# Gating of a mixture of experts on one core: fewer small instructions, one-hot sets ahead of turns, the last tile turned in pieces

## The chip, the cores and the metric

The kernel runs on one core of a Trainium2 chip. A core has a matrix engine, TensorE (PE, with its weight loads, PEld), a vector engine, VectorE (DVE), ScalarE (ACT), GpSimd (POOL), and SyncE (SP), which only issues DMA transfers here. Each engine works through its own queue in order. [...] The metric is the time of one execution on the device, in microseconds (us), lower is better.

## What is computed

Two layers on an input of 4 x 16 x 16 positions with 1024 channels, that is 1024 tokens, all in float32. Layer 0 is a lambda convolution (not touched here). Layer 1 is attention with 16 heads of 64 over each batch entry's 256 tokens, and behind it a mixture of 8 experts, to whose gating the change belongs:

```python
gate_logits = jax.nn.softmax(x @ gate_w + gate_b, axis=-1)
selected = (gate_logits >= THRESHOLD).astype(x.dtype)     # 0.1
weights = gate_logits * selected
wsum = jnp.sum(weights, axis=-1, keepdims=True)
weights = weights / jnp.where(wsum == 0, jnp.ones_like(wsum), wsum)
for e in range(E):                                        # 8 experts, 1024 x 1024 each
    out = out + weights[:, e:e + 1] * (x @ expert_w[e] + expert_b[e])
```

Here x is the layer norm of the attention's result, and the sum over the experts is added to that result.

## The kernel before

The 1024 tokens are eight row tiles of 128. The attention ends with an output projection, `project_out(t, j)`: for row tile t and column half j it runs eight matmul steps, one per 128 channels (each is two instructions on PE, since the data are float32), and then DVE adds the result to the tile `xs[t]` (L922). Between the steps the gating is woven in by hand. A counter, `chunks`, counts the steps: 9 to 16 belong to tile 3, 17 to 32 to tile 4, 33 to 48 to tile 5, 49 to 64 to tile 6, 65 to 80 to tile 7. The table `at_chunk` (L1357) says after which step which stages are emitted, as pairs (stage, tile). The order of each engine's queue is the order in which the program emits (`tc.manual_schedule()`).

The stages of a tile are:

- Stage 0, `normalise` (L1147): statistics on DVE, one square root on ACT; for tiles 0 to 5 ACT writes the normalised row, SP stores it to a scratch `rows` in DRAM and fetches it back as four quarters; for tiles 6 and 7 DVE writes it in two halves (L1166). SP also stores `xs[t]` to `out`.
- Stage 1, `turn_rows` (L1170): the row transposed. Tiles 0 to 5 by one DVE transpose of the quarters (L187), which waits for their DMA; tiles 6 and 7 by eight PE transposes into two PSUM banks and two ACT copies (L1179, L1180), and then an ACT copy and an SP store that put the row into `rows`.
- Stages 2 to 5 work on a batch of tiles at once: (0, 1, 2), (3, 4, 5), (6), (7). Stage 2, `gate_sums`: 16 PE instructions per tile and one DVE copy. Stage 3, `gate` (L1205): PE's `pg`, then on DVE the copy of the token numbers into `listed`, bias, maximum, and Exp on ACT. Stage 4, `thresholds` (L1228): ten small DVE instructions. Stage 5, `place` (L1243): on PE a prefix sum over tokens, `pp` (L1250, L1251), on DVE the place of each token in its expert's list.
- Stage 6, `entries_of` (L1264), for each tile: two sets of one-hot rows on DVE (`one0`, `one1`, L1268) and two products with token number and weight (`entry`, L1276), on POOL for tiles 0 to 5 and on DVE for 6 and 7. The buffers of each of these are two deep.
- Stage 7, `enter` (L1285): 16 PE instructions that add the tile's entries into the lists, which lie in two PSUM banks under the tag `sc`.

After step 80 the list of expert 0 alone is copied and spread over the partitions (`copy_lists`, `spread_lists`, `take_lists`), seven `warm` matmuls keep PE going (L1420), and stages 0 and 1 of tile 7 follow, with a load of the Exp table between them. Then tile 7 is put through expert 0 as a whole (`weighted`, the "dense" product, 16 steps), while stages 2 to 6 of tile 7 are emitted between its steps, and POOL gathers the rows of expert 0. During the first seven products of expert 0 (L1516) come stage 7 of tile 7, the copy of all lists, and after product 4 `last_lists` (L1429): the spreads `pc`, two counts `pn` and `pn0`, and DVE's copies into `gather`, `slot` and `add`. PSUM banks of the tags `mm` and `tr` are rings of three each; `pc`, `pn`, `pn0` and the odd products take theirs from `tr`. Then come the products of the other experts, and what is left over.

Of the kernel before, what the change touches and what calls it, by code (L numbers as in the profile page):

```python
# [32 lines left out]
F32 = mybir.dt.float32  # L33
# [6 lines left out]
P = 128  # L40
# [16 lines left out]
E = 8  # L57
# [12 lines left out]
def kernel(  # L70
# [1027 lines left out]
    with ExitStack() as gating:  # L1098
# [40 lines left out]
        nc.vector.memset(kept[:, 0, :], 0.0)  # L1139

# [6 lines left out]
        def normalise(t):  # L1147
# [10 lines left out]
            if t < NT - 2:  # L1158
                normalised(row, xs[t], mv[:, 0:1], rstd)
                nc.sync.dma_start(rows[ts(t, P), :], row)  # L1160
                row = l2w.tile([P, Q, C // Q], F32, tag="xg", name=f"quarters{t}")
                quarters_of(rows[ts(t, P), :].rearrange("n (f c) -> n f c", f=Q), row)
            else:
                for j in range(2):
                    half = slice(j * HALF, j * HALF + HALF)
                    nc.vector.tensor_scalar(row[:, half], xs[t][:, half], mv[:, 0:1], rstd, ALU.subtract, ALU.mult)  # L1166
# [3 lines left out]
        def turn_rows(t, row):  # L1170
# [5 lines left out]
            for j in range(2):  # L1176
                pt = tr(f"row{t}_pt{j}")
                for c in range(4):
                    nc.tensor.transpose(pt[:, ts(c, P)], row[:, (4 * j + c) * P : (4 * j + c + 1) * P], ident)  # L1179
                nc.scalar.copy(row_T[:, 4 * j : 4 * j + 4, :], pt.rearrange("p (c n) -> p c n", c=4))  # L1180
# [6 lines left out]
            return row_T  # L1187
# [17 lines left out]
        def gate(tiles, sums):  # L1205
# [3 lines left out]
            for i in range(n):  # L1209
                nc.tensor.matmul(pg[:, ts(i, E)], sums[:, ts(i, P)], quarters, start=True, stop=True)  # L1210
            listed = of_tiles("listed", n, E, 2)
            nc.vector.tensor_copy(
                listed[:, :, :, 0], token[:, tiles[0] : tiles[0] + n].unsqueeze(2).to_broadcast([P, n, E])
            )
            weight = listed[:, :, :, 1]
            top, fix, keep = of_tiles("g_top", n), of_tiles("g_fix", n), of_tiles("g_keep", n, E)
# [4 lines left out]
            if n == 1:  # L1221
                nc.scalar.activation(weight, weight, AF.Exp, bias=top)
            else:
                nc.vector.tensor_add(weight, weight, top.unsqueeze(2).to_broadcast([P, n, E]))
                nc.scalar.activation(weight, weight, AF.Exp)
            return listed, top, fix, keep

        def thresholds(listed, top, fix, keep):  # L1228
            weight = listed[:, :, :, 1]
            all_of = top.unsqueeze(2).to_broadcast([P, top.shape[1], E])  # L1230
            nc.vector.tensor_reduce(top, weight, AX.X, ALU.add)
            nc.vector.reciprocal(top, top)
            nc.vector.tensor_mul(weight, weight, all_of)
            nc.vector.tensor_scalar(keep, weight, THRESHOLD, None, ALU.is_ge)
            nc.vector.tensor_mul(weight, weight, keep)
            nc.vector.tensor_reduce(top, weight, AX.X, ALU.add)
            nc.vector.tensor_scalar(fix, top, 0.0, None, ALU.is_equal)
            nc.vector.tensor_add(top, top, fix)
            nc.vector.reciprocal(top, top)
            nc.vector.tensor_mul(weight, weight, all_of)  # L1240
            return listed, keep

        def place(tiles, listed, keep):  # L1243
# [11 lines left out]
            nc.vector.tensor_scalar(slot, keep, -1.0, 1.0, ALU.mult, ALU.add)  # L1255
            nc.vector.tensor_mul(slot, slot, from_end[:, t0 : t0 + n, :])
            nc.vector.tensor_add(slot, slot, pp.rearrange("p (n e) -> p n e", n=n))
            at = l2w.tile([P, 3, n, E], I32, tag="at", name=f"at{t0}", padded_shape=[P, 3, 3, E])
            nc.vector.tensor_copy(at[:, 0, :, :], slot)
            nc.vector.tensor_scalar(at[:, 1, :, :], at[:, 0, :, :], 31, None, ALU.bitwise_and)  # L1260
            nc.vector.tensor_scalar(at[:, 2, :, :], at[:, 0, :, :], 5, None, ALU.logical_shift_right)
            return at, listed

        def entries_of(t, i, at, listed):  # L1264
# [10 lines left out]
            for k in range(2):  # L1275
                (nc.vector if t >= NT - 2 else nc.gpsimd).tensor_mul(  # L1276
                    entry[:, :, k, :], column, listed[:, i, :, k].unsqueeze(2).to_broadcast([P, E, 32])
# [25 lines left out]
        def spread_lists(a, entries):  # L1303
            pc = tr(f"pc{a}").rearrange("p (e i s) -> p e i s", e=E, i=2)
# [32 lines left out]
        def stage(n, t):  # L1337
# [11 lines left out]
            elif n == 5:  # L1349
                placed[t] = place(tiles, *gated[t])  # L1350
            elif n == 6:
                entered[t] = entries_of(t, t - tiles[0], *placed[tiles[0]])
# [16 lines left out]
            46: ((6, 1),),  # L1369
            47: ((1, 4),),  # L1370
            48: ((7, 0), (6, 2)),
            50: ((7, 1), (0, 5)),
            53: ((7, 2),),
# [6 lines left out]
            74: ((3, 6), (6, 4)),  # L1380
            75: ((7, 3), (4, 6), (6, 5)),
            76: ((7, 4),),
            77: ((5, 6), (6, 6)),
            78: ((7, 5),),
# [24 lines left out]
        with tc.manual_schedule():  # L1409
# [6 lines left out]
            pc = spread_lists(0, entries)  # L1416
# [5 lines left out]
            load_table(AF.Exp)  # L1422
            take_lists(0, 1, pc)
            stage(1, NT - 1)

# [3 lines left out]
        def last_lists(entries):  # L1429
            take_lists(1, E, spread_lists(1, entries))  # L1430


            pn = tr("pn")
            nc.tensor.matmul(pn[:, :E], ones, kept[:, NT, :], start=True, stop=True)
            need = l2.tile([P, E], F32, tag="need", name="need")
            nc.vector.tensor_copy(need, pn[:, :E])
            pn0 = tr("pn0")
            nc.tensor.matmul(pn0[:, :2], ones, kept[:, NT - 1, :: E - 1], start=True, stop=True)
            nc.vector.tensor_scalar(need[:, :: E - 1], pn0[:, :2], float(LEFT), None, ALU.add)
# [150 lines left out]
        with tc.manual_schedule():  # L1590
            entries, last_rows = [], []
            last_row_T = two.tile([P, NC, P], F32, tag="last_row_T", name="last_row_T", bufs=1)
            nc.scalar.copy(last_row_T, turned_rows[NT - 1])
# [156 lines left out]
```

## Time and profile before

| | us |
|---|---|
| median of 3 runs | 1225.91 (1224.85 to 1229.62) |
| the profiled execution, its own time | 1227.45 |
| its span, first to last instruction | 1225.6 |
| busy, TensorE | 1208.7 |
| busy, VectorE | 721.4 |
| busy, GpSimd | 401.5 |
| busy, ScalarE | 203.8 |
| mean granted clock of TensorE | 0.997 of full |

The span has one profiled execution, with times from its start. Step 9 begins at about 657 us, step 65 ends at 714.6, step 80 at about 735.3; dense runs from 739.8 to 755.1, expert 0 from there. Busy time of an engine counts instructions at work; the idle time in front of an instruction is given with what released it. The end of a matmul is modelled, so a run of matmuls is drawn slightly longer than the next one's start would allow.

### The profile page before, as it was taken

To read this page: it belongs to the slowest core of one execution; us is meant where nothing else is said; L and a number is where in the kernel's file an instruction comes from. 1 tells how busy PE (TensorE), PEld (TensorE's weight loads), DVE (VectorE), ACT (ScalarE), POOL (GpSimd) and SP (SyncE) were. 2 spreads that over 40 slices of the span, in tenths; PEclk is the share of its full clock that TensorE was granted. 3 is DMA by queue.
4 is the path that set the end of the run, shared out by engine and by line. 5 is a ranking of instruction groups with operands and counts; after the bars stand their busy time and mean duration, and the time that the engine had idled before them with its cause. 6 is when DMAs were issued, how large, how long until landed. Compare 5 with 4: busy or idle time off the path is not lost.

```text
span 1225.6 us, 13283 instructions
## 1 busy us (share of the span) xinstructions
PE 1208.7 (99%) x4780; PEld 632.8 (52%) x4780; DVE 721.4 (59%) x1274; ACT 203.8 (17%) x502; POOL 401.5 (33%) x467
## 2 busy tenths in 40 slices
PE   9999999999999999999999999999999999999998
PEld 5444884778884444444444444444344334434443
DVE  5796636668332666565644567666566655565742
ACT  3310111111001222121311212101111111111110
POOL 1051351364000122222232116427443635363521
PEclk9999999999999999999999999999999999999999
DMA  9102014772201353525465646564855576556432
GB/s 349 27 1 69 18 44 123 248 251 94 69 9 60 104 172 104 170 95 181 147 213 192 206 172 238 143 185 95 246 158 141 109 230 182 144 138 180 98 82 55
DMA packets 94121, 169.77 MB, mean 139 GB/s; under 512 B 11968, under 2 KB 48848, under 8 KB 94048
## 3 DMA queue, kind: packets, MB, share of 16 engines
q1 hardware_dynamic: 73600, 108.49, 26.8%
q0 software_dynamic: 16144, 51.45, 17.3%
q10 hardware_dynamic: 4304, 8.91, 2.1%
q8 instruction: 40, 0.66, 0.2%
q14 instruction: 33, 0.27, 0.1%
HBM read 116.12 MB, written 48.50 MB: 134 GB/s over the span
## 4 chain that ended last, share of the span: by engine, by line
PE 87%; DMA 7%; DVE 3%; SPq 2%; issue 1%; ACT 1%; POOL 0%; DVEq 0%; POOLq 0%; ACTq 0%
PE p L1516 31%; PE pqk L665 15%; PE pv L665 7%; PE po L920 5%; PE pq_pair L400 4%; PE left L1558 3%; PE pq L319 3%; PE pT L510 3%; DMA ln_rows<-ln_rows 2%; PE pk L431 2%; PE sc L824 2%; PE pa L893 2%; PE rest L1572 2%; PE pv L538 2%; DMA quarters<-rows 1%; DMA s<-two_T 1%
## 5 line engine op out<-in xcount | busy, mean ns | idle before, releaser
L1041 POOL DMA_INDIRECT w_e_xg<-rows,gather x146 | 156.3, 1071 | 50.9 <-issue 41.4
L1516 PE MATMUL p<-w_e,A 128*128 128x512 f32 x368 | 163.2, 593 | 1.3 <-DVE slot L1328 1.3
L865 POOL TENSOR_TENSOR s_q<-s_q,total 128x128 f32<-128x128 f32 (+1 forms) x128 | 60.2, 506 | 276.5 <-DVE total L862 276.5
L920 PE MATMUL po<-w_p,y_T 128*128 128x512 f32 x256 | 116.8, 607 | 0.0
L1516 PEld LDWEIGHTS p<-w_e,A 128*128 128x128 f32 x368 | 69.6, 190 | 89.9 <-issue 89.0
L1064 POOL DMA_INDIRECT out_dram<-y,add x32 | 56.5, 1766 | 177.5 <-ACT y L1522 114.3
L1516 PE MATMUL p<-T,S 128*128 128x512 f32 x256 | 112.7, 593 | 0.0
L1522 ACT ACTIVATE y<-y,slot 128x512 f32<-128x512 f32 x64 | 46.2, 723 | 333.1 <-DVE y L1530 177.9
L665 PE MATMUL pqk<-ln,w_qk 128*128 128x512 f32 x192 | 85.7, 595 | 0.0
L1516 PEld LDWEIGHTS p<-T,S 128*128 128x128 f32 x256 | 48.6, 190 | 60.8 <-issue 60.5
L850 ACT ACTIVATE s_q<-sc,top 128x128 f32<-128x128 f32 (+1 forms) x128 | 52.1, 420 | 164.4 <-DVE top L846 140.6
L920 PEld LDWEIGHTS po<-w_p,y_T 128*128 128x128 f32 x256 | 47.6, 192 | 54.5 <-issue 53.5
L187 DVE STREAM_TRANSPOSE A<-w_e_xg 128x1024 f32<-128x1024 f32 x32 | 39.7, 1240 | 47.2 <-DMA w_e_xg<-rows,gather 47.2
L665 PEld LDWEIGHTS pqk<-ln,w_qk 128*128 128x128 f32 x192 | 36.1, 190 | 43.7 <-issue 41.9
L665 PE MATMUL pqk<-T,S_qk 128*128 128x512 f32 x128 | 57.8, 595 | 0.0
L1516 PE MATMUL p<-T,A 128*128 128x512 f32 x128 | 57.5, 592 | 0.0
L1516 PE MATMUL p<-w_e,S 128*128 128x512 f32 x128 | 57.5, 592 | 0.0
L665 PE MATMUL pv<-w_v,ln 128*128 128x256 f32 x192 | 43.7, 380 | 1.5 <-ACT ln L223 1.1
L319 PE MATMUL pq<-w_q,xn 128*128 128x512 f32 x96 | 44.5, 599 | 0.3 <-ACT xn L299 0.3
L1558 PE MATMUL left<-w_e,one 128*32 128x512 f32 x312 | 41.8, 593 | 0.0
L1516 PEld LDWEIGHTS p<-w_e,S 128*128 128x128 f32 x128 | 24.3, 190 | 30.6 <-issue 30.1
L1516 PEld LDWEIGHTS p<-T,A 128*128 128x128 f32 x128 | 24.3, 190 | 30.6 <-issue 30.1
(329 smaller groups left out, 1846.5 us busy)
## 6 DMA issues: line engine op xcount, KB each, us to landing
w_e<-in_expert_w_dram SPq DMA_DIRECT2D x12, 2048.0 KB, 15.2
s_rows<-s_q SPq DMA_DIRECT2D x32, 384.0 KB, 2.3
s_rows<-s_rows SPq DMA_DIRECT2D x128, 96.0 KB, 2.3
w_qk<-in_W_attnT_dram SPq DMA_DIRECT2D x8, 1024.0 KB, 5.4
w_e<-in_expert_w_dram ACTq DMA_DIRECT2D x4, 2048.0 KB, 9.5
xn<-in_xT_dram SPq DMA_DIRECT2D x8, 512.0 KB, 7.2
w_q<-in_Wq_dram SPq DMA_DIRECT2D x16, 256.0 KB, 7.3
x_at<-in_x_dram POOLq DMA_DIRECT2D x8, 512.0 KB
```

The lines of the kernel that those rows point to most:

```text
L187: nc.vector.transpose(row_T[:, :, :slots].rearrange("p c (g j) -> p g c j", j=32), row[:, : slots // 32, :].rearrange("p g (c i) -> p g c ...
L319: nc.tensor.matmul(pq, xn[:, c, ts(t, P)], w_q[kc][:, c, :], start=(c == 0), stop=(c == NC - 1))
L400: nc.tensor.matmul(bank, a[:, c, :], b[:, c, :], start=(c == 0), stop=(c == NC // 2 - 1))
L665: nc.tensor.matmul(bank, stationary(c), moving(c), start=(c == 0), stop=(c == NC // 2 - 1))
L850: nc.scalar.activation(blocks(h, qt), psc[:, h, cols].rearrange("p (b f i) -> p b f i", f=Q, i=32), AF.Exp, bias=top[:, qt, h : h + 1], sc ...
L865: nc.gpsimd.tensor_mul(blocks(h, qt), blocks(h, qt), total[:, qt, h : h + 1].unsqueeze(2).unsqueeze(3).to_broadcast([P, 1 + qt, Q, 32]),)
L920: nc.tensor.matmul(po, y_T[:, c, ts(t, P)], w_p[j][:, c, :], start=(c == 0), stop=(c == NC - 1))
L1041: nc.gpsimd.indirect_dma_start(out=row[:, g, :], out_offset=None, in_=table[: (TOK - P) * Q, :] if e in SHORT else table, in_offset=bass.I ...
L1064: nc.gpsimd.indirect_dma_start(out=out[: TOK - P, :] if e in SHORT else out, out_offset=bass.IndirectOffsetOnAxis(ap=add[:slots, e, k : k ...
L1516: nc.tensor.matmul(bank, a[:, c, :], b[:, c, :], start=(c == 0), stop=(c == NC // 2 - 1))
L1522: nc.scalar.mul(y[i][:, ts(j, HALF)], y[i][:, ts(j, HALF)], slot[:, e, 1, 2 * pair + i : 2 * pair + i + 1])
L1558: nc.tensor.matmul(bank[ts(i, 32), :], stationary, w[of][j][:, c, :], start=(c == 0), stop=(c == NC - 1))
```

## The change

It has four parts.

1. Fewer instructions. The tile `listed` is made once for all tokens, and its token numbers are written once at set-up, so stage 3 loses its token copy. In `thresholds` the test for a zero sum and the addition become one instruction; for a batch of one tile the sum of the exponentials comes from ACT's Exp itself (`accum_out`), and scaling with the test or the product becomes one instruction. In `place` four instructions become two, the second of which writes integers at once.
2. Order. The one-hot sets of tile 2 go from step 48 to step 46, in front of stage 7 of tile 0; the turn of row 4 goes from step 47 to 52, behind the norm of row 5. The sets of tiles 4 and 5 both go to step 74, in front of stage 7 of tile 3 and the thresholds of tile 6. Stage 7 of tile 4 goes from 76 to 77, of tile 5 from 78 to 79.
3. The last tile. DVE writes the normalised row in three pieces (256, 256 and 512 columns). Stage 1 turns only the first half, in two pairs of transposes into one bank with an ACT copy behind each pair; the second half is turned behind step (0, 1) of dense. The row's store and the copy `last_row_T` go behind step (0, 3), stages 2, 3 and 4 one step later each, and the load of the Exp table behind stage 1.
4. Lists. In `last_lists` `pc`, `pn` and `pn0` lie in the two banks of the tag `sc`, which the lists leave free, and both counts are formed before `take_lists`.

```diff
+        listed = l2.tile([P, NT, E, 2], F32, tag="listed", name="listed")
+        nc.vector.tensor_copy(listed[:, :, :, 0], token.unsqueeze(2).to_broadcast([P, NT, E]))
...
-                for j in range(2):
-                    half = slice(j * HALF, j * HALF + HALF)
-                    nc.vector.tensor_scalar(row[:, half], xs[t][:, half], mv[:, 0:1], rstd, ALU.subtract, ALU.mult)
+                cuts = (0, M, HALF, C) if t == NT - 1 else (0, HALF, C)
+                for some in (slice(a, b) for a, b in zip(cuts, cuts[1:])):
+                    nc.vector.tensor_scalar(row[:, some], xs[t][:, some], mv[:, 0:1], rstd, ALU.subtract, ALU.mult)
...
+            if t == NT - 1:
+                pt = tr(f"row{t}_pt0")
+                for a in (0, 2):
+                    turn_chunks(pt, row_T, row, 0, a, a + 2)
+                return row_T
+            turn_half(t, row_T, row, 0)
+            turn_half(t, row_T, row, 1)
+            store_row(t, row)
+            return row_T
+
+        def turn_chunks(pt, row_T, row, j, a, b):
+            for c in range(a, b):
+                nc.tensor.transpose(pt[:, ts(c, P)], row[:, (4 * j + c) * P : (4 * j + c + 1) * P], ident)
+            nc.scalar.copy(
+                row_T[:, 4 * j + a : 4 * j + b, :], pt[:, a * P : b * P].rearrange("p (c n) -> p c n", n=P)
+            )
+
+        def turn_half(t, row_T, row, j):
+            turn_chunks(tr(f"row{t}_pt{j}"), row_T, row, j, 0, 4)
...
-                nc.scalar.activation(weight, weight, AF.Exp, bias=top)
+                total = of_tiles("g_top", n)
+                nc.scalar.activation(weight, weight, AF.Exp, bias=top, accum_out=total)
+                return weight, total, keep
...
+        def thresholds(weight, top, keep):
+            n = top.shape[1]
+            all_of = top.unsqueeze(2).to_broadcast([P, n, E])
+            if n > 1:
+                nc.vector.tensor_reduce(top, weight, AX.X, ALU.add)
+            nc.vector.reciprocal(top, top)
+            if n == 1:
+                of = weight[:, 0, :]
+                nc.vector.tensor_scalar(keep[:, 0, :], of, top, THRESHOLD, ALU.mult, ALU.is_ge)
+                nc.vector.scalar_tensor_tensor(of, of, top, keep[:, 0, :], ALU.mult, ALU.mult)
             else:
...
             nc.vector.tensor_reduce(top, weight, AX.X, ALU.add)
+            nc.vector.scalar_tensor_tensor(top, top, 0.0, top, ALU.is_equal, ALU.add)
             nc.vector.reciprocal(top, top)
             nc.vector.tensor_mul(weight, weight, all_of)
...
-            nc.vector.tensor_scalar(slot, keep, -1.0, 1.0, ALU.mult, ALU.add)
-            nc.vector.tensor_mul(slot, slot, from_end[:, t0 : t0 + n, :])
-            nc.vector.tensor_add(slot, slot, pp.rearrange("p (n e) -> p n e", n=n))
+            nc.vector.scalar_tensor_tensor(slot, keep, 0.0, from_end[:, t0 : t0 + n, :], ALU.is_equal, ALU.mult)
...
-            nc.vector.tensor_copy(at[:, 0, :, :], slot)
+            nc.vector.tensor_add(at[:, 0, :, :], slot, pp.rearrange("p (n e) -> p n e", n=n))
...
-            46: ((6, 1),),
-            47: ((1, 4),),
-            48: ((7, 0), (6, 2)),
+            46: ((6, 1), (6, 2)),
+            48: ((7, 0),),
             50: ((7, 1), (0, 5)),
+            52: ((1, 4),),
             53: ((7, 2),),
...
-            74: ((3, 6), (6, 4)),
-            75: ((7, 3), (4, 6), (6, 5)),
-            76: ((7, 4),),
-            77: ((5, 6), (6, 6)),
-            78: ((7, 5),),
+            74: ((3, 6), (6, 4), (6, 5)),
+            75: ((7, 3), (4, 6)),
+            77: ((7, 4), (5, 6), (6, 6)),
+            79: ((7, 5),),
             80: ((7, 6),),
...
             stage(0, NT - 1)
-            load_table(AF.Exp)
             take_lists(0, 1, pc)
             stage(1, NT - 1)
+            load_table(AF.Exp)
...
-            take_lists(1, E, spread_lists(1, entries))
-            pn = tr("pn")
-            nc.tensor.matmul(pn[:, :E], ones, kept[:, NT, :], start=True, stop=True)
+            spreads = ps.tile([P, 2, HALF], F32, tag="sc", name="spreads", bufs=1)
+            pc, pn, pn0 = spreads[:, 0, :], spreads[:, 1, :E], spreads[:, 1, E : E + 2]
+            pc = spread_lists(1, entries, pc)
+            nc.tensor.matmul(pn, ones, kept[:, NT, :], start=True, stop=True)
+            nc.tensor.matmul(pn0, ones, kept[:, NT - 1, :: E - 1], start=True, stop=True)
+            take_lists(1, E, pc)
...
-            nc.scalar.copy(last_row_T, turned_rows[NT - 1])
...
-                    (0, 2): lambda: stage(2, NT - 1),
-                    (0, 4): lambda: (stage(3, NT - 1), first_sum(0)),
-                    (0, 6): lambda: stage(4, NT - 1),
+                    (0, 1): lambda: turn_half(NT - 1, turned_rows[NT - 1], normal[NT - 1], 1),
+                    (0, 3): lambda: (
+                        stage(2, NT - 1),
+                        store_row(NT - 1, normal[NT - 1]),
+                        nc.scalar.copy(last_row_T, turned_rows[NT - 1]),
+                    ),
+                    (0, 5): lambda: (stage(3, NT - 1), first_sum(0)),
+                    (0, 7): lambda: stage(4, NT - 1),
```

## The prediction

> **What bounds the kernel now.** I read the page's busy line first, then TensorE's list of waits, then the stretches around those waits in the timeline, the table by stretches (with the clock), and the chain of waits.
>
> ```profile
> PE 1208.7 (99%) x4780; PEld 632.8 (52%) x4780; DVE 721.4 (59%) x1274; ACT 203.8 (17%) x502; POOL 401.5 (33%) x467
> ```
>
> TensorE (PE) is busy for 99% of the span, so only three things can shorten the run: PE work left out, PE idle time, PE at a lower clock. The change leaves out no PE work (as many transposes, gate matmuls and spreads as before). The list of waits, cut to 640 to 800 us where the edited code runs:
>
> ```profile
> PE lists L1287 <- POOL entry L1276: 2.8, 3, 1.9
> PE p L1516 <- DVE slot L1328: 1.3, 1, 1.3
> PE pc L1307 <- DVE entries L1298: 0.5, 1, 0.5
> PE dense_pe L1056 <- ACT row_T L1180: 0.2, 1, 0.2
> ```
>
> These 4.9 us are all the idle time that the edits can reach directly. The longest wait, in the timeline:
>
> ```profile
> 698.82 1.25 DVE L187 STREAM_TRANSPOSE row_T<-quarters 128x1024 f32<-128x1024 f32 x1 [4.90 <-DMA quarters<-rows]
> 699.98 0.72 DVE L1268 TENSOR_TENSOR one<-count,at 128x256 f32<-128x256 int32 x2
> 700.85 1.20 POOL L1276 TENSOR_TENSOR entry<-one,listed 128x256 f32<-128x256 f32 x2 [5.29 <-DVE one L1268]
> 702.10 0.43 PE L1287 MATMUL lists<-entry,one 128*32 128x64 f32 x16 [1.85 <-POOL entry L1276]
> ```
>
> VectorE (DVE) stands 4.90 us at the turn of row tile 4, whose DMA is late; tile 2's one-hot sets stand behind it in the queue, POOL's products behind those, and PE behind POOL. What follows is in the table by stretches (length, busy us of PE, weight load, DVE, ACT and POOL, then PE's clock, DMA share, GB/s):
>
> ```profile
> 700.20:702.10 1.90, 0.04 (x1) 0.00 (x1) 1.90 (x5) 0.00 (x0) 1.20 (x2) 1.00 0.02 4
> 703.60:707.10 3.50, 3.50 (x5) 1.37 (x5) 0.25 (x1) 1.24 (x1) 0.00 (x0) 0.51 0.37 150
> 707.10:710.50 3.40, 3.40 (x9) 1.52 (x8) 0.44 (x1) 0.00 (x0) 0.00 (x0) 1.00 0.50 127
> ```
>
> Just behind that gap PE runs 3.5 us at half clock: five matmuls against nine in the next stretch. The chain gives the price in its line for the 24 matmuls behind the gap:
>
> ```profile
> 702.53 12.19 PE po L920 x24
> 775.50 14.83 PE p L1516 x34
> ```
>
> Late in the run 224 matmuls take 96.33 us in the chain, 0.43 each, so 24 need 10.32: 1.87 us were lost to the clock. The second line shows that the 1.3 us wait for slot at 774 to 775 had no such sequel (34 x 0.43 = 14.6).
>
> **The change part by part.**
>
> *One-hot sets ahead of the turn* (tiles 0 to 2). Tile 2's sets go to chunk 46, the turn of row 4 behind them to chunk 52. The buffers for the sets are two deep, so tile 2's wait for the lists matmuls of tile 0 (end at 695.2); two sets of 0.38 give 696.0, POOL's two products 1.20 more after its four of 692.91 to 695.56, so 697.3. PE asks at 700.24: no wait. Queued behind the waiting sets on DVE are the add of po (5,1), due at 694.8, and row 5's norm, which now comes before the turn: add 0.68, statistics and scalars some 2.7 (as 700.62 to 703.40 shows), so about 699.2 instead of 703.4; then the turn, whose DMA landed at 698.7. Nobody waits for those adds before chunk 56. SP's queue: row 5's store and four quarter loads go out 4 us earlier, into the free stretch behind the first half of w0. From store issue to landing took 704.91 to 712.41, 7.5 us; now 700.4 to 707.9, plus 1.25 of turn, against 710.5 where PE takes the gate sums. The cover is 1.4 us. Gain: the gap of 1.85, and 0.26 that the modelled end of the last matmul hides (six matmuls drawn as 2.84, six times 0.43 is 2.58): 2.11. With it the half-clock stretch: 1.87.
>
> The row says that an idle 1.9 us precedes half clock. [...]
>
> *Fewer small instructions.* For a batch of three tiles DVE loses the token copy 0.14, the fix 0.17, one of the place steps 0.17 and the cast 0.18; a single tile also loses one reduce 0.16 and one of two products, 0.17 to 0.51: 0.7 and about 1.1, twice each, 3.5 us of DVE in all. Added: one token copy at set-up (0.19, as the 128x64 row of from_end), hidden, since PE waits for nothing there; if DVE were the limit it would cost 0.19. The sum that rides on the single tile's Exp is bounded by 0 and by the 0.20 of ACT's smallest instruction; it lies beside DVE's other work; I take 0. This pays only where DVE is on the path: the chain runs through DVE from 725.1 to 735.5. There go out 0.18 (cast) + 0.28 (token copy) + 0.16 + 0.51 + 0.15 + 0.17 + 0.28 = 1.73. Against it stands the new order: tile 5's sets now stand before tile 6's thresholds and wait for tile 3's lists matmuls, some 0.3 to 0.5; so the last add of po comes 1.2 to 1.4 earlier. PE's own side: the waits 0.50 and 0.43 plus 0.27 and 0.24 of hidden ends give 1.44, because (7,4) and (7,5) are asked one chunk (0.86) later while POOL is served earlier. The smaller counts: 1.2. The 0.5 us wait for entries stays, since they come behind the same add.
>
> *Spreads in the lists' banks.* At 774 PE waits for DVE's four slot copies, since pc, pn and pn0 take three of three banks of one ring and the next product needs pc's. In the lists' banks, which were read at 769.66, they block nobody: 1.32. Behind it DVE's add, row sums and next add stay where they were, but DVE idles 1.62 and 2.74 soon after (before L1536 and L1524), so it takes up the 1.3.
>
> *Last tile turned in pieces.* Before: eight transposes from 738.49, dense at 739.79. PE is held until 738.5 by the warm matmuls, so the shorter first norm piece (some 0.27 instead of 0.50) gains nothing. After: two transposes end at 738.9; the ACT copy of 256 columns, an estimate from 0.59 for 512 and 1.06 for 1024, is 0.35; dense could start at 739.28, and four transposes at 0.13 that move into it bring this to 739.80: even. But the second pair writes the bank that the copy reads. Nearest row: PE held by a tile's readers (slot, above). If it waits, it comes after 739.28, 0.26 later. Ends 0 and -0.3; I take -0.27. [...] The Exp table (1.28) now loads between the copies of the first and second half; dense's chunks 0 to 3 (3.4 us) cover it, else it would cost up to 1.28. Tile 7's gate comes a chunk later: keep ready at about 749.1, PE asks at 749.0 to 749.5; 0 to -0.2, taken as 0. The row store moves 2 us back on SP; the gathers that need row 7 begin at 780.
>
> Sum: 2.11 + 1.87 + 1.2 + 1.32 - 0.27 = 6.2 us. Behind 782 PE runs without a wait to the end, so all of it reaches the end. The profiled execution took 1227.45 (span 1225.6), so it would be 1221.2; it stands 1.5 above the median of 1225.91, against which I give 1219.7. If the median run had no half-clock stretch (1.5 is near 1.87), it would be 1221.6.
>
> **The rivals.**
>
> *The half clock is not the gap's.* The other gaps (0.5, 0.4, 1.3) show no such stretch, so size may decide, or phase. If it stays, or the median never had it: 6.2 - 1.87 = 4.3, 1221.6. For it: the 1.5 above. Against: it follows the gap at once and nothing like it stands elsewhere in the stage. [...]
>
> *The stalls only move.* If writes into the one shared listed tile wait for POOL's reads of other tiles' part, tile 6's thresholds wait until POOL's last product (about 730.7), and the 1.2 is gone (1220.9); the gate's prefix matmul, which PE asks for at 730.3, then idles about 1.0 as well: 1221.9. Against: PE began row 7's transposes at 738.49 while DVE still wrote that row's other half until 738.79, so parts of a tile are told apart.
>
> *Slower: row 5's turn becomes the wait.* Place: the gate sums at chunk 65. Row 4's quarters took 8.8 us to land under w0's stream. If row 5's store meets the same, PE idles by what exceeds the 1.4 of cover and falls to half clock again. It decides from 1.4 + 6.2 - 1.87, some 5.7 us late; slower by 0.5% from 12 late, 1232 or more. Against: the stream's second half starts only at 718.46.
>
> **How the numbers follow.** A measurement here tells about 0.5%, 6.1 us; faster begins at 1219.8. Main case 0.70, 1217.8 to 1221.3 (hidden ends larger or pieces free at the low end, pieces and gate at the high end): 0.45 faster, 0.25 within. Half clock 0.12 and moved stalls 0.07, all within. Slower rival 0.11: 0.10 beyond, 0.01 within. So 0.45, 0.45, 0.10. The range 1217.6 to 1224.0 leaves out the slower rival and the tails.
>
> **What would show it.** The clock at 1.00 in every stretch from 690 to 720, and no PE wait for lists before tile 3; none for slot at the spread; the last add of po 1.2 earlier behind DVE work that is some 20 instructions shorter; between the two pairs of row 7's transposes a gap of 0.3 or none. Wrong it would be with a PE wait for parts at chunk 65, for the DVE queue behind tile 5's sets, or for the table load inside dense.

## The result, and the profile after

The changed kernel takes 1222.99 us (median, 1220.28 to 1226.77), against 1225.39 for the kernel before, timed beside it: a ratio of 0.9982, 95% interval 0.9974 to 0.9991. That is 2.2 to 2.4 us where 6.2 were forecast. (One of the 20 executions of the kernel before took 2127.33 us and is left out of the ratio.) The time itself lies inside the forecast range, the gain is little over a third of the forecast one. The profiled execution took 1225.42 (span 1223.6), 2.0 less than that of before.

The busy line of the page of after (in this part and those below, the line numbers of the changed kernel are up to 17 higher than before's, and the experiments differ by a few more):

```profile
PE 1208.8 (99%) x4780; PEld 632.7 (52%) x4780; DVE 719.4 (59%) x1256; ACT 203.9 (17%) x505; POOL 404.7 (33%) x467
```

The work of PE is the same to 0.1 us. DVE has 18 instructions fewer and 2.0 us less to do. TensorE's list of waits, of after (what it waited for, us in total, times, longest):

```profile
PE pq L339 <- DVE average L250: 1.6, 1, 1.6
PE pc L452 <- DVE s L460: 1.3, 1, 1.3
...
PE pT L510 <- ACT two_T L518: 0.8, 1, 0.8
PE pv L665 <- DMA w_v<-in_W_attnT_dram: 0.6, 1, 0.6
...
PE pc L1324 <- DVE entries L1315: 0.5, 1, 0.5
...
PE row_pt L1190 <- ACT row_T L1191: 0.5, 1, 0.5
...
PE pp L1269 <- DVE g_keep L1250: 0.3, 1, 0.3
```

Of the four waits that the forecast showed, three are gone (2.8 for the lists, 1.3 for slot, 0.2 for row_T); the 0.5 for entries is still there, as said. New are 0.5 for row_T (the bank that the pieces of the last tile share) and 0.3 for g_keep (tile 7's gate). The lines from layer 0 and the attention (L452, L510, L665) are longer than before's 0.9, 0.4 and 0.4, in code that the change leaves alone.

The place of the longest wait, in the timeline of after (start, us, engine, line, operation):

```profile
698.33 0.76 DVE L1285 TENSOR_TENSOR one<-count,at 128x256 f32<-128x256 int32 x2 [1.56 <-PE lists L1304]
...
699.23 1.20 POOL L1293 TENSOR_TENSOR entry<-one,listed 128x256 f32<-128x256 f32 x2 [0.82 <-DVE one L1285]
...
703.24 0.43 PE L1304 MATMUL lists<-entry,one 128*32 128x64 f32 x16
...
710.51 1.25 DVE L187 STREAM_TRANSPOSE row_T<-quarters 128x1024 f32<-128x1024 f32 x1 [3.34 <-DMA quarters<-rows]
```

Tile 2's sets now wait only 1.56 us for a buffer, POOL is done at 700.4, and PE reaches tile 2's lists at 703.24 with no idle time in front (no bracket on that line). Row 5's turn waits for its DMA on an idle DVE and ends at 711.76, while PE takes the gate sums at 714.17. The clock there, in the table by stretches (length, busy us of PE, weight load, DVE, ACT, POOL, then PE's clock, DMA share, GB/s):

```profile
700.00:703.00 3.00, 3.00 (x23) 1.33 (x22) 2.51 (x7) 1.18 (x2) 0.43 (x1) 1.00 0.55 186
703.00:706.00 3.00, 3.00 (x23) 1.48 (x23) 0.31 (x1) 0.27 (x1) 0.00 (x0) 1.00 0.44 175
```

Full clock, and in the chain of waits the same 24 matmuls cost 10.50 instead of 12.19:

```profile
703.67 10.50 PE po L920 x24
```

So in the edited code nearly everything came as forecast, and yet the execution is only 2.0 us shorter. To see why, the run is cut at PE's first instruction of each kind, read from TensorE's timeline (us, each profiled execution; "e1" is before again, "e2" after again, see below):

| stretch | before | after | e1 | e2 |
|---|---|---|---|---|
| start to step 9 (untouched code) | 655.76 | 658.82 | 656.98 | 652.25 |
| lists of tile 0 to gate sums of tile 3 | 19.88 | 16.27 | 17.95 | 16.26 |
| gate sums of tile 3 to the first spread | 21.69 | 20.60 | 21.68 | 20.61 |
| first spread to dense | 3.45 | 3.15 | 3.45 | 3.16 |
| dense to first product of expert 0 | 15.28 | 16.37 | 15.28 | 15.62 |
| to the sixth product (behind the spreads) | 20.43 | 18.97 | 20.43 | 18.97 |
| the rest | 450.15 | 450.42 | 450.53 | 450.62 |

(The stretch from step 9 to tile 0's lists, 39.01 in all, is left out. "Step 9" is here, and wherever a stretch is counted from it, the place where PE takes up the projection for the last time, two steps or 1.7 us ahead of step 9 itself; what lies between is untouched too.) From step 9 to the sixth product the profiled pair gains 5.37; ahead of step 9, where both kernels are the same, it loses 3.06; at the end 0.27. The 3.06 has two visible parts in the trace of after. One is the longer waits above, with one of 0.4 more (L665 for DVE's ln) and a 0.3 shorter one: 1.1 together. The other is a stretch of half clock behind two short gaps (0.54 and 1.06), worth some 1.7 (3.41 us at half the clock), which before's trace does not have at this place:

```profile
277.00:280.50 3.50, 1.86 (x10) 1.24 (x10) 2.31 (x4) 3.50 (x7) 0.00 (x0) 0.95 0.77 234
280.50:284.00 3.50, 3.50 (x10) 2.81 (x10) 0.00 (x0) 0.22 (x2) 0.00 (x0) 0.56 0.89 318
```

In before the second row holds 18 matmuls at clock 1.00, here 10 at 0.56. That the place of the half clock can move from one execution to another is what the experiments then were about.

### The profile page after: what moved, and what is told of

It reads as the page before. It is cut to its first block, busy times and chain, and to the rows that moved or that the text cites. A ratio compares the mean times of both kernels' runs of the same rounds, so it can differ in the third digit from the quotient of the medians.

```text
span 1223.6 us, 13265 instructions
## 1 busy us (share of the span) xinstructions
PE 1208.8 (99%) x4780; PEld 632.7 (52%) x4780; DVE 719.4 (59%) x1256; ACT 203.9 (17%) x505; POOL 404.7 (33%) x467
## 4 chain that ended last, share of the span: by engine, by line
PE 90%; DMA 5%; DVE 2%; SPq 2%; issue 1%; ACT 0%; POOL 0%; DVEq 0%; POOLq 0%; ACTq 0%
PE p L1533 31%; PE pqk L665 15%; PE po L920 8%; PE pv L665 7%; PE pq_pair L400 4%; PE left L1575 3%; PE pq L319 3%; PE pT L510 3%; DMA ln_rows<-ln_rows 2%; PE pk L431 2%; PE sc L824 2%; PE pa L893 2%; PE rest L1589 2%; PE pv L538 2%; DMA s<-two_T 1%; PE last_pe L1696 1%
## 5 line engine op out<-in xcount | busy, mean ns | idle before, releaser
L665 PE MATMUL pqk<-ln,w_qk 128*128 128x512 f32 x192 | 85.7, 595 | 0.0
L665 PEld LDWEIGHTS pqk<-ln,w_qk 128*128 128x128 f32 x192 | 36.1, 190 | 43.7 <-issue 42.1
L665 PE MATMUL pqk<-T,S_qk 128*128 128x512 f32 x128 | 57.8, 595 | 0.0
L665 PE MATMUL pv<-w_v,ln 128*128 128x256 f32 x192 | 45.4, 391 | 2.1 <-ACT ln L223 1.1
L665 PEld LDWEIGHTS pv<-w_v,ln 128*128 128x128 f32 x192 | 37.4, 197 | 8.4 <-ACT ln L223 1.3
L880 DVE STREAM_TRANSPOSE s_T<-s_rows 128x768 f32<-128x768 f32 x32 | 30.3, 964 | 17.8 <-DMA s_rows<-s_rows 17.8
```

Source lines behind the costliest of these rows:

```text
L665: nc.tensor.matmul(bank, stationary(c), moving(c), start=(c == 0), stop=(c == NC // 2 - 1))
```

## The experiments

Two theories. *The path* (B in the expectations): the gain is what the stage table shows, term by term; the half clock behind the gap is drawn anew in each execution, so its 1.87 are seldom there to be had. *The gap's clock* (the forecast; A in the expectations): the idle 1.85 us trip the clock each time, and something in the change gives gain back, the last tile's pieces first of all. A third: an untouched stage reacts to the change.

### Both kernels again

**Before once more.** No edit.

> The kernel before, unchanged, looked at again with the granted clock of every run. Theory A (the half-clock stretch belongs to the gap in front of tile 2's lists matmuls, in every execution): the profile shows again a gap of about 1.9 us there, half clock for 3.4 us behind it, and from the lists matmuls of tile 0 to the gate sums of tiles 3 to 5 again 19.9 us; nearly all runs show a mean clock of 0.997 to 0.998. [...]

1224.92 us, a ratio of 0.9992 (0.9981 to 1.0004) to before: the measure is honest to about 0.1%. Its list of waits and its stretches behind the gap:

```profile
PE lists L1287 <- POOL entry L1276: 2.5, 3, 1.6
```

```profile
700.00:705.00 5.00, 3.39 (x24) 1.49 (x23) 4.16 (x10) 0.59 (x2) 1.20 (x2) 1.00 0.02 7
705.00:710.00 5.00, 5.00 (x13) 2.13 (x13) 0.69 (x1) 0.86 (x1) 0.00 (x0) 1.00 0.32 113
```

The same kernel, the same gap of 1.6 us, and full clock behind it. Its one half-clock stretch stands at 278 to 282.

**After once more**, on the same chip, and later on two others.

> The changed kernel, unchanged, looked at again. Theory A (it has lost about 3 us ahead of the gating in every execution): step 9 of the projection begins again at about 659 us, with half clock at about 288 us, and its runs have a clock of 0.998. Theory B (lottery): step 9 begins anywhere from 655 to 659 us, half clock at 288 in a part of the runs only; from step 9 to product 5 of expert 0 it takes 114.4 us again, within 0.5.

> The changed kernel a third time. By its stages (113.6 to 114.4 us from step 9 to product 5 against 117.3 to 119.7 before) it should gain 3.2 to 4.2 us, and some 0.5 more for the half-clock stretch that it can no longer have behind tile 2's lists: 0.9962 to 0.997. If the first measurement (0.9982) is the rule, its runs lie around 1222 to 1223 and the loss stands ahead of step 9; if the second (0.9955), around 1219 to 1220.

> The changed kernel a fourth time: 0.9955 to 0.997, as by its stages. If the first measurement is as frequent as the later ones, 0.998.

| | us | ratio to before, timed beside it |
|---|---|---|
| first measurement | 1222.99 | 0.9982 (0.9974 to 0.9991) |
| second (e2) | 1219.53 | 0.9955 (0.9939 to 0.9970) |
| third (e9) | 1220.86 | 0.9960 (0.9946 to 0.9974) |
| fourth (e13) | 1221.65 | 0.9964 (0.9951 to 0.9976) |

The three later ones agree with each other (4.4 to 5.5 us), and their ratios lie beyond the first one's interval. The stages of the edited code are the same in all four profiles to 0.1 us, but for one (dense to product 0, below). What differs is the untouched part: step 9 begins at 652.25, 656.15 and 655.18 in the later three, 658.82 in the first. In e2's list of waits those for s, two_T and w_v are missing altogether, and so is the stretch of half clock at 277 to 284; in e9 that stretch is there, from 277.5. The third theory, an untouched stage that reacts to the change, is not borne out: over all 17 profiles of this document step 9 begins between 652.25 and 658.82, mixed for kernels with the edits and without them, and the first profile of after has it latest of all.

### Is the half clock the gap's?

**The gap doubled**: on before, row 4's turn is done three times over (the repeats change no value).

```diff
             turn(row_T, row)
+            if t == 4:
+                turn(row_T, row)
+                turn(row_T, row)
```

> The kernel before with the DVE turn of row 4 done three times (the two repeats change nothing in the result), so that PE's gap in front of tile 2's lists matmuls grows from 1.6 to 1.9 by 2.5, to about 4.2 us. If half clock follows idle time once enough of some window is idle, it now follows in every run: the stage from tile 0's lists matmuls to the gate sums takes 16.3 + 4.2 + 1.9 = 22.4 us, and every run has a mean clock of 0.998 or less. If the stretch is unconnected with the gap, the stage takes 20.5 us, and the clocks are spread as before (0.997 to 1.000). Time: 3 to 5 us above the kernel before.

1227.70 us, 1.0034 (1.0017 to 1.0050). Its longest wait and its stretches:

```profile
PE lists L1290 <- POOL entry L1279: 5.1, 3, 4.1
```

```profile
698.00:702.00 4.00, 0.00 (x0) 0.00 (x0) 3.97 (x7) 0.00 (x0) 1.16 (x2) 1.00 0.00 0
702.00:703.50 1.50, 1.41 (x19) 0.79 (x20) 1.13 (x5) 0.20 (x1) 0.04 (x1) 0.95 0.00 0
703.50:707.00 3.50, 3.50 (x6) 1.48 (x5) 0.05 (x1) 1.24 (x1) 0.00 (x0) 0.53 0.37 150
```

PE idle for 4.1 us, half clock some 1.3 us after the work resumes, for 3.4 us. Tile 0's lists to the gate sums of tile 3 take 22.15 us where 22.4 were expected: 16.27, the gap, and 1.76. And all ten executions of this kernel had a mean clock of 0.998 or less, against 26 of 87 of the kernel before over four measurements. So in this kernel idle time does bring the half clock, at 4.1 us in the profile and, by their mean clocks, in all ten executions, at 1.2 to 1.9 only now and then: of the five profiles that have before's ordinary gap (before, e1, e4, e5, e11) one, the one that I forecast from, shows a stretch behind it; of the eleven profiles without the gap, none.

The clock of the traces shows more. In the six traces with a stretch ahead of the end, its beginning and the fall of the clock at the end are whole numbers of 3.41 us apart: in before (703.64 and 1222.47) 152.00 such windows, in after (280.15 and 1222.22) 276.00, in e1, e7, e9 and e11 277.0, 152.0, 276.0 and 181.0. So in each of them the falls lie on one grid of 3.41 us that runs through the execution. Where the grid lies differs from one execution to the next: counted back from the fall at the end, the border at which PE's instructions rise from 6 to 8 in a us to some 10 (the clock column shows 1.00 from the start) stands between 4.5 (e9) and 7.6 us (e11). Laid into the windows of the grid, the doubled gap and then the gap of before look so (columns as above):

```profile
696.53:699.94 3.41, 1.44 (x4) 0.37 (x2) 3.34 (x3) 0.00 (x0) 0.00 (x0) 1.00 0.02 7
699.94:703.36 3.42, 1.27 (x18) 0.76 (x19) 3.07 (x9) 0.20 (x1) 1.20 (x2) 1.00 0.00 0
```

```profile
700.23:703.64 3.41, 1.55 (x20) 0.95 (x20) 2.96 (x9) 0.20 (x1) 1.20 (x2) 1.00 0.01 2
```

The half clock comes with the next window, at 703.36 and at 703.64. Over all windows of the 17 profiles from that border on, each one with 2.1 us or more of idle PE time (2.15 in the doubled gap, the others behind the last matmul) was followed by half clock, and none with less than 1.6. Between 1.6 and 2.0 both happened: half clock behind 1.64 (at 277 in after, and the like within 0.01 in e1 and e9), 1.86 (before's gap) and 1.89 (two gaps at 602 to 605 in e11), none behind 1.68 (the gap in e4) or 1.97 (the first window above). In before the window opened at 700.23 and the gap at 700.25, so the whole gap fell into one window; in e1 a border cut the gap of 1.6, and 1.13 was the larger part.

What a stretch costs can be read from the same 87 executions: those with a mean clock of 0.999 take 1223.7 us in the mean, those at 1.000 1224.2, those at 0.996 to 0.998 1226.4 to 1228.7, some 2 to 5 more (one stretch or several, and the waits ahead of them).

### One part alone, or one undone

**The order of steps 46 to 52 alone**, on before; and **that order undone**, on after.

```diff
-            46: ((6, 1),),
-            47: ((1, 4),),
-            48: ((7, 0), (6, 2)),
+            46: ((6, 1), (6, 2)),
+            48: ((7, 0),),
             50: ((7, 1), (0, 5)),
+            52: ((1, 4),),
```

> The kernel before with one edit: tile 2's one-hot sets ahead of the turn of row 4, and this turn behind the norm of row 5. Both theories: the stage from tile 0's lists matmuls to the gate sums of tiles 3 to 5 takes 16.3 us at full clock. Theory A: 0.9968 of the time before (4.0 us), since gap and stretch go in every run. Theory B: 0.998 to 0.9995 (0.6 to 2.4 us), since the gap is often shorter than in the one profile and the stretch rarely there.

> The changed kernel with that one edit taken back; all others stay. Theory A: the gap of 1.9 us and the stretch return, 4.0 us more than the changed kernel, so 1.0015 of the kernel before. Theory B: a gap of 0 to 2 us returns, the stretch in a part of the runs; 0.5 to 2.4 us more than the changed kernel, 0.9985 to 1.000 of the kernel before.

Alone: 1222.87 us, 0.9980 (0.9968 to 0.9991). Undone: 1223.09, 0.9987 (0.9973 to 1.0000). Both lie where *the path* had them, not at the 0.9968 and 1.0015 of *the gap's clock*. Their waits for the lists, of the first and of the second:

```profile
PE lists L1287 <- POOL entry L1276: 0.9, 2, 0.5
```

```profile
PE lists L1304 <- POOL entry L1293: 1.7, 1, 1.7
```

The wait of 1.2 to 1.9 us belongs to this edit and to nothing else; the 0.9 that stays (0.5 and 0.43, as in before; here at 724 and 727) belongs to the other part. In the stage table, lists of tile 0 to gate sums of tile 3: 16.27 with the new order, 18.01 with the old one and everything else changed. The gain is the wait and hardly anything more (17.95 - 16.27 = 1.68 for a wait of 1.6; 1.74 for 1.7): of the hidden 0.26 that I added for the drawn end of the last matmul only 0.07 was there. The two ratios multiplied give 0.9967, about the whole change as measured later.

**The lists' banks alone**, on before.

```diff
-            take_lists(1, E, spread_lists(1, entries))
+            spreads = ps.tile([P, 2, HALF], F32, tag="sc", name="spreads", bufs=1)
+            pc, pn, pn0 = spreads[:, 0, :], spreads[:, 1, :E], spreads[:, 1, E : E + 2]
...
+            take_lists(1, E, pc)
```

> The kernel before with one edit: pc, pn and pn0 in the lists' two banks. No wait of PE for slot; from the first product of expert 0 to its sixth 18.97 us instead of 20.43, as in the changed kernel. If the wait only moved, PE would stand at a later product for the add that reads product 4, and the time from the sixth product to the end, 450.1 to 450.7 us in all six profiles so far, would grow by up to 1.3 us.

1222.61 in one execution. The wait for slot is gone, and the stretch to the sixth product is 18.97 against 20.43: 1.46, and 450.45 from there to the end against 450.15 to 450.53 before. Nothing of it comes back. The gap before tile 2's lists was 1.2 us here, with the old order:

```profile
PE lists L1287 <- POOL entry L1276: 2.1, 3, 1.2
```

So the size of that gap is drawn too: it goes by when row 4's quarters land. In all five profiles that have it, it is 2.2 us less than the time from tile 0's lists to the start of row 4's turn (4.05 in before, 3.42 here).

**The shorter instructions alone**, on before (stages 3 to 5 as in after, everything else old), and **the order of steps 74 to 80 undone**, on after.

```diff
-            74: ((3, 6), (6, 4), (6, 5)),
-            75: ((7, 3), (4, 6)),
-            77: ((7, 4), (5, 6), (6, 6)),
-            79: ((7, 5),),
+            74: ((3, 6), (6, 4)),
+            75: ((7, 3), (4, 6), (6, 5)),
+            76: ((7, 4),),
+            77: ((5, 6), (6, 6)),
+            78: ((7, 5),),
```

> The kernel before with the shorter gate code alone; order of stages, last tile and lists' banks as before. If shorter DVE work makes the gain between the gate sums of tiles 3 to 5 and the spread of list 0 (21.7 us before, 20.6 after), it is here too: 20.6 to 20.8, with at most 0.3 of waits for lists. If the order of the sets makes it, 21.4 to 21.7 with the waits of 0.5 and 0.4 still there. The first wait (1.2 to 1.9 us for tile 2) stays in both cases.

> The changed kernel with steps 74 to 79 in their order of before (tile 5's sets behind the thresholds of tile 6, stage 7 of tiles 4 and 5 a step earlier). If shorter DVE work makes the gain in that stretch: 20.6 to 20.8 us. If the order makes it: 21.4 to 21.7, with PE waiting twice for POOL.

1225.78 and 1222.66, one execution each; here the stages speak. Gate sums of tile 3 to the first spread: 21.69 before, 21.10 with the shorter instructions alone, 21.07 with all but the late order, 20.60 with both. For this stage the two kernels are the same case, the shorter instructions with the old late order: 0.6 of the 1.1 come from leaving out small instructions, 0.5 more from the order on top of it. What the late order gives without the shorter instructions no run shows. Both keep the same wait for the lists there:

```profile
PE lists L1299 <- POOL entry L1288: 1.7, 2, 1.5
```

```profile
PE lists L1304 <- POOL entry L1293: 0.3, 1, 0.3
```

(In the first the 1.5 is the gap behind tile 1; of the later ones 0.28 is left, as in the second.)

### The last tile

After's timeline at row 7's transposes, of TensorE and of ScalarE:

```profile
736.72 0.39 PE L1190 MATMUL row_pt<-ident,row 128*128 128x128 f32 x2
737.58 0.44 PE L1190 MATMUL row_pt<-ident,row 128*128 128x128 f32 x2 [0.46 <-ACT row_T L1191]
737.85 1.88 PE L1056 MATMUL dense_pe<-w_e,row_T 128*128 128x512 f32 x4
```

```profile
737.15 0.37 ACT L1191 COPY row_T<-row_pt 128x256 f32<-128x256 f32 x1 [1.24 <-PE row_pt L1190]
```

The second pair does wait for the copy out of the same bank. **Two banks**, on after: the second pair writes a bank of its own.

```diff
-                pt = tr(f"row{t}_pt0")
-                for a in (0, 2):
+                for a, pt in ((0, tr(f"row{t}_pt0")), (2, mm(f"row{t}_pt1"))):
                     turn_chunks(pt, row_T, row, 0, a, a + 2)
```

> The changed kernel with the second pair of the last tile's transposes in a bank of its own. If the bank that ACT reads holds the pair back (0.5 us of wait in the list), the wait goes, and from the spread of list 0 to the first product of expert 0 it takes 18.5 us instead of 18.8 (3.16 + 15.62), some 0.2 staying as a wait of dense for the first copy. If something else holds it, it stays at 18.8.

The wait is gone, and the 0.2 wait of dense for row_T, which before had, is back in its place:

```profile
PE dense_pe L1056 <- ACT row_T L1190: 0.2, 1, 0.2
```

First spread to dense takes 2.88 instead of 3.16, dense to product 0 15.72 instead of 15.62: 0.17 net. 1219.29 us, 0.9955 (0.9940 to 0.9971), the lowest median of all kernels here, but not to be told from after by time (0.9955 to 0.9964 on the three chips).

In the first profile of after, dense to product 0 took 16.37, 0.75 more than in its three others. The rows of tile 7's gate, of after first and of e2 below it:

```profile
741.82 0.64 PE L1212 MATMUL parts<-row_T,gw 128*32 128x128 f32 x16
...
744.01 0.29 DVE L1216 COPY sums<-parts 128x128 f32<-128x128 f32 x1 [5.67 <-remote]
...
748.55 0.36 PE L1269 MATMUL pp<-g_keep,before 128*128 128x8 f32 x2 [0.27 <-DVE g_keep L1250]
```

```profile
735.26 0.64 PE L1212 MATMUL parts<-row_T,gw 128*32 128x128 f32 x16
...
735.97 0.29 DVE L1216 COPY sums<-parts 128x128 f32<-128x128 f32 x1 [4.21 <-PE parts L1212]
```

In e2 DVE copies the gate sums 0.71 us after PE begins them, in after 2.19, with DVE idle; all of tile 7's gate comes that much later, and PE, which asks for it one step behind, has to wait (0.27 of it as a wait in the list, the rest behind the drawn ends of matmuls). Before's copy was late too (1.46 behind the beginning of the sums) and cost nothing. What held DVE there no trace says. It was late in four more profiles, those of e9, e10, e11 and e12 (1.40 to 1.58), which ran on one chip, and in none of the other eleven, with 0.71 each.

**The gate's step one earlier**, on two banks: stage 3 of tile 7 behind step (0, 4), as far from the sums as it was before.

```diff
-                    (0, 5): lambda: (stage(3, NT - 1), first_sum(0)),
+                    (0, 4): lambda: (stage(3, NT - 1), first_sum(0)),
```

> The changed kernel with the second pair of the last tile's transposes in its own bank, and tile 7's gate put one step earlier, behind step (0, 4) of dense, with its thresholds left behind (0, 7). From the spread of list 0 to the first product of expert 0: 18.4 us, no wait for row_T but 0.2 of dense's, and no wait for keep even where DVE is late. Time 0.3 us under the changed kernel, which alone can't be told from it.

```profile
PE pg L1226 <- DVE sums L1215: 0.2, 1, 0.2
```

Dense to product 0 becomes 16.21, 0.5 worse: PE asks for `pg` before DVE has copied the sums, and DVE was late here (1.58 us behind the beginning of the sums). 1220.32 us, 0.9965 (0.9953 to 0.9978). After itself, as late on the same chip (e9, 1.42), takes 15.62. So after's step is the better one when DVE is that late; what the earlier step does with DVE on time no run shows.

### Can the half clock at 277 be filled away?

Three kernels set idle PE time ahead of the layer norm's turn to work on matmuls whose results nobody reads: into a bank that ScalarE was still reading, then two into a free bank and four behind it, then the latter with two banks for row 7.

```diff
+        def keep_busy(bank, n):
+            for _ in range(n):
+                nc.tensor.matmul(bank[:, :P], ident, ident, start=True, stop=True)
...
+        keep_busy(banks[0], 2)
         turn_on_pe(ln_rows[:, (NT - 1) % 3, :], banks)
+        keep_busy(tr("spare"), 4)
```

> The changed kernel with eight matmuls without use laid into the two waits of PE at 274 to 280 us (0.5 and 1.1 us), three ahead of the last transposes of layer 0's end, five behind them. If idle time makes the stretch at 280, no profile and no run shows one: all clocks 0.999 or 1.000, no run above 1222, and a median 0.5 to 1 us under that of the changed kernel, since a third to a half of its runs have the stretch. If the stretch is not idle time's doing, a third of the runs still has 0.998.

> The changed kernel with PE kept busy in its waits at 274 to 280 us: two matmuls without use into the bank that the last transposes of layer 0's end write next, four behind them into a bank of their own. If idle time in one window makes the stretch at 277 to 284, no run shows it: no clock under 0.999, and a median 0.3 to 0.8 us under the changed kernel's beside it. If not, a fifth to a third of the runs has 0.998.

> The same with the second pair of the last tile's transposes in a bank of its own: a further 0.2 us (113.45 instead of 113.63 from step 9 to product 5), 0.995 to 0.9965 of the kernel before, ahead of both kernels if the fillers do what is expected.

1222.50 us (0.9983, 0.9971 to 0.9995), 1221.91 (0.9969, 0.9957 to 0.9981) and 1222.96 (0.9980, 0.9968 to 0.9991): no better than after, and the first and third rather worse. In all of them the filler itself waited, in the first and in the second as follows:

```profile
PE ln_two L729 <- ACT ln L223: 2.2, 1, 2.2
```

```profile
PE spare L731 <- ACT ln L223: 1.1, 1, 1.1
```

None of the three profiles has a stretch at 277, but neither have those of e2 and e13, and two of e8's and three of e15's twelve executions still had a clock of 0.997 or 0.998. The test says nothing on the cause: the longer of the two gaps that it was to fill stayed, though the shorter one (0.5) is gone from the lists.

## Why the prediction was wrong, and where it was right

Undisturbed profiles, term by term (us gained):

| term | forecast | measured |
|---|---|---|
| gap before tile 2's lists | 2.11 | 1.29 to 1.74 (1.85 in before's own profile) |
| half clock behind it | 1.87 | 1.69 to 1.76 in before's own profile; 0 in e1, e4, e5, e11 |
| shorter instructions and late order | 1.2 | 1.08 |
| lists' banks | 1.32 | 1.46 |
| last tile in pieces | -0.27 | -0.05 (3.16 + 15.62 against 3.45 + 15.28) |
| sum | 6.2 | 3.8 to 4.2 without a stretch |

**The step that failed** is "With it the half-clock stretch: 1.87". The mechanism was there: 3.61 between before's profile and after's in that stage are 1.85 and 1.76 (1.69 by the chain, 12.19 against 10.50; I had set 10.32 for the undisturbed 24 matmuls), and the doubled gap shows idle time to be the cause. But I took an event of one execution for a cost of each. The runs show it in one of the five profiles with the ordinary gap, so its mean is about 0.35. The hint was in my own text, in that none of the other gaps had such a sequel and the profiled execution stood 1.5 above the median; I gave the case 0.12 and should have made its 4.3 us, or 1221.6, the main forecast: the stage sum (3.8 to 4.2) and three of four measurements of the ratio (4.4 to 5.5) stand near it. Its heading ("the half clock is not the gap's") is refuted all the same; the "size or phase" that it named is what the windows show.

What the runs show of the stretch: its length is 3.41 us in the clock of the traces each time, and it begins at a border of the grid. 1.64 us of idle time in a window were enough three times, 2.1 us or more in every window that had them, less than 1.6 in none. Two windows of 3.41 share a gap of 4.1 so that one of them has 2.05 of it or more, which fits all ten executions of the doubled gap; a gap of 1.85 falls into one window as a whole only sometimes. What decides between 1.6 and 2.0 is not shown.

**The gap** was mis-sized: a hidden end of 0.26 of which 0.07 existed, and a length that depends on when row 4's DMA lands (1.2, 1.5, 1.6, 1.7, 1.9 in five profiles). The rest of that paragraph stood: no wait on tile 2's sets, norm ahead of the turn, row 5's store and loads unhindered (store at 703.29, quarters landed at 710.5, 7.2 us where 7.5 were forecast). The **slower rival** is refuted by the same rows: the turn ends 2.4 us before PE takes its sums.

**Shorter instructions**: right in size (1.2 and 1.08) and in kind, for the two waits of 0.9 vanished; e11 and e12 show that without the late order 0.28 of them would have stayed. DVE's busy time fell by 2.0 us, where I had counted 3.5 less 0.19. The rival that stalls only move is refuted. **Lists' banks**: right (1.32 and 1.46), and nothing returned behind it.

**Last tile**: the bank wait came as forecast (0.46, copy 0.37 where 0.35 was estimated), and two banks take it away: the pair that writes one half of the bank waited 0.46 us for ACT's copy out of the other half, and in e6, with a bank of its own, it has no wait. Dense starts 0.3 earlier, and the four transposes in it cost 0.34 to 0.44 instead of the 0.52 (four of 0.13) that I took. What I called 0 to -0.2 for tile 7's gate was right for three of four profiles of after and cost 0.75 in the first.

**What stays open** is why the first measurement shows 2.2 us and the later ones 4.4 to 5.5. In the first one's profile 3.06 us were lost ahead of step 9 and 0.75 at tile 7's gate, which would do; but a profile is one execution, and the same 20 executions lie 2 us higher than the later ones even at a like mean clock (at 0.999: 1222.3 against 1220.2, which is 1219.4, 1220.2 and 1221.4 on the three chips), so it is not the half clock alone. Whether the chip, the placement in memory or the change decides when the DMAs of the untouched part land was not tried. The interval of each of the four lies under 1, so the changed kernel is faster; by its stages alone it is so by 0.3 to 0.35%.

**The best version** is two banks: 113.45 us from step 9 to the sixth product against 113.63, 1219.29 us, 0.9955 (0.9940 to 0.9971) to before.

## What to carry to other kernels

Price what a queue order costs by the wait that stands in the trace; price a stretch of half clock only after several profiles of the same kernel have shown it at the same place. When the untouched part of a kernel varies by more than the edit is worth (652 to 659 us here, for 4 us of edit), cut the profiles at fixed instructions and compare stages, which repeat to 0.1 us. Do not put work that a busy engine asks for behind work that waits for a DMA (1.68 us here), and give a product that is read late a bank that lies free anyway, not one of a ring from which the next matmul takes its own (1.46 us here).

## What the runs showed of the hardware

- In each of the six traces with a half-clock stretch ahead of the end, the falls of TensorE's clock lay on a grid of 3.41 us. Over the 17 profiles half clock followed each window of it with 2.1 us or more of idle time, some of those with 1.6 to 2.0 (1.86 in before's gap; two gaps that add up to 1.64 at 277 in after), and none with less. The stretch of 3.41 us at half clock in before cost 1.69 to 1.76 us of matmul time.
- All 17 profiles end at half clock too, from 2.1 (e7) to 5.4 us (e13) after the last matmul on, where no matmul follows.
- The sum that rides on an Exp was not free on ScalarE: in after's trace the 128x8 Exp of 0.30 us is followed at 727.06 by an ACTIVATION_READ_ACCUMULATOR of 0.18 us, in place of a reduce of 0.15 us on DVE (at 728.37 in before). ScalarE had the idle time there (4.39 us in front of that Exp).
- The same kind of DMA, a row's quarters back from DRAM, took 3.2 us from the last of its four issues to the turn that waited for it for row 5 in after (707.28 to 710.51), and 8.9 for row 4 in before (689.88 to 698.82), beside a weight load (issued at 687.10, 11.2 us to landing; DMA share 0.98 from 690 to 695 and 0.88 from 695 to 699); the latter decided the size of the gap.
